# The first column of a scan's input: from VectorE to GpSimd and ScalarE

## The chip, the core and the metric

The kernel runs on one core of a Trainium2 chip. A core has TensorE (PE, matmuls; PEld is its weight load), VectorE (DVE), ScalarE (ACT), GpSimd (POOL) and SyncE (SP), whose queue issues the DMA transfers. Each engine works through its own queue in order. The metric is the time of one execution on the device in microseconds (us).

## The reference

Two layers work on 4 images of 64 x 64 tokens with 256 channels. The first is a Mamba block, the second an SSD block followed by a mixture of 8 experts. What matters here is the recurrence of the first, for 512 channels d and 16 states n:

```python
dt = softplus(dbl[..., :16] @ dt_w.T + dt_b)      # (B, L, 512)
dA = exp(dt[..., None] * A)                       # A = -exp(A_log), (512, 16)
h  = dA * h + (dt * x)[..., None] * B[:, None, :] # over the 4096 tokens of an image
y  = einsum('bdn,bn->bd', h, C)
```

The term that is added in each step is u B with u = dt * x. Where the tokens are cut into chunks, the first step of a chunk also needs dA * h of the last token of the chunk before.

## The kernel before

The program has three stages: *mixers* (both recurrent blocks, 64 chunks of 256 tokens, 16 to an image), *experts* and *turn*. Only the mixers are changed.

**Units.** Channels and states of a chunk are cut into 16 units, unit u = 4 j + f with j over four groups of 128 channels and f over four groups of states. A tile of a unit is 128 partitions (32 channels x 4 states) by four rows of 256 tokens. A unit's steps in `scan` are these:
- `da`, on ACT: four exps of 255 columns each (column 0 of each row stays 0, which starts a row anew), into one of three fixed tiles.
- `ub`, on DVE: the product of `u4` (u, loaded for each j) and row B of `bc4[f]` (B and C, loaded for each f at the chunk's start, five buffers), into a PSUM tile with a single buffer.
- In all chunks but an image's first (60 of 64), a small addition on DVE: `e0[:, :, f]`, what the states bring along, is added to column 0 of the four rows of `ub`. `e0` is made for each j, four units at a time: a product on POOL, exp on ACT, and a product with the last states of the chunk before (`hlast`) on POOL.
- `h`, on DVE: one scan over all 1024 columns.
- `hlast`, on ACT: a copy of the last column of each row of `h`.
- `p`, on POOL: `h` times row C of `bc4[f]`.
- `py`, on PE: the sum over states, added in PSUM to D times the passed-on x, which ACT writes first from `gx`. After two j the result is multiplied on DVE by the other half of `gx`, the gate.

**Order.** Nothing of this is issued as written. `Plan` records each operation with a slot (`k_.at(n)`: n units from the chunk's first) and its dependences, where two uses of parts of a tile that do not meet are independent. `Plan.order` then fills the queues by simulating them with weights written by hand: on each engine, of the operations that are ready and whose buffers have room, the lowest slot goes first. The instructions are issued in that order; the tile framework beneath adds the semaphores. While the scan of chunk i runs, other steps run beside it: `front0` and `mid0` of a later chunk, `tail0`, `front1`, `ssd` and `back1` of earlier ones. `BEHIND` is the planner's delay between an operation and one that depends on it on the same engine.

**Silus.** In the trace an ACT_TABLE_LOAD stands ahead of ACT's Silus and another behind them (x256 in all, mean 1283 ns): `silus` runs the Silus (and a Tanh) of a tile or two and then loads the set with exp and log again. `Plan.acts` records all of these as one operation, which nothing can come between. This happens twice a chunk.

Of the kernel before, what the change touches and what calls it, by code (L numbers as in the profile page):

```python
# [14 lines left out]
AF = mybir.ActivationFunctionType  # L15
ALU = mybir.AluOpType
# [4 lines left out]
P = 128  # L21
T = 256
# [4 lines left out]
KC = C // P  # L27
KD = DI // P
NST = 16
SQ = 4  # L30
# [14 lines left out]
AHEAD = 4  # L45
# [77 lines left out]
class Op:  # L123
    def __init__(self, seq, engine, slot, step):
        self.seq, self.engine, self.slot, self.step = seq, engine, slot, step
        self.calls, self.weight, self.lag = [], 0.0, 0.0
        self.port = self.scan = self.ride = False
        self.behind = self.issued = None
        self.deps, self.users, self.roots = set(), [], []
        self.start = self.end = None  # L130
# [6 lines left out]
class Plan:  # L137
# [4 lines left out]


    SIGNAL = {"DVE": 0.13, "ACT": 0.19, "PE": 0.21, "POOL": 0.12}
    BEHIND = {"DVE": 0.13, "ACT": 0.14, "PE": 0.0, "POOL": 0.13}
    LANES = 8
    SPARE = {}
    PATIENCE = 4.0
# [69 lines left out]
    def act(self, out, src, func, **kw):  # L218
        aps = sum(isinstance(v, Part) or hasattr(v, "ap") for v in kw.values())
        w = 0.06 + self.width(out) / 1130 + 0.09 * aps  # L220
        self.note("ACT", w, self.nc.scalar.activation, (out, src, func), kw, (out,), (src, *kw.values()))

    def copy(self, out, src):
        self.note("ACT", 0.05 + self.width(out) / 1200, self.nc.scalar.copy, (out, src), {}, (out,), (src,))

    def acts(self, weight, calls):

        key = object()
        for f, args, out, src in calls:
            self.note("ACT", weight, f, args, {}, (out,) if out is not None else (), (src,), join=key)  # L230

    def dve(self, name, *args, **kw):
        out, *rest = (*args, *kw.values())
# [41 lines left out]
    def order(self):  # L275
# [19 lines left out]
        lanes, landings = ("SP",), []  # L295
        done = 0
        scan = before = last = shared = None

        def room(op, now):
            for root in op.roots:  # L300
# [9 lines left out]
        while done < len(self.ops):  # L310
            if not events:
                left = [o for o in self.ops if o.start is None and not o.missing][:20]
                raise RuntimeError("no order: " + str([(o.engine, o.slot, [r.ring for r in o.roots]) for o in left]))
            now = heappop(events)
            while events and events[0] <= now:
                heappop(events)
            for e in engines:
                while waiting[e] and waiting[e][0][0] <= now:
                    _, _, op = heappop(waiting[e])
                    insort(could[e], (op.slot, op.seq, op))  # L320
                if free[e] > now or e in lanes and len(landings) >= self.LANES and landings[-self.LANES] > now:
                    continue
                for i, (_, _, op) in enumerate(could[e]):

                    if op.ride and not (scan and now - scan.start < 0.2) and now - op.ready < self.PATIENCE:
                        continue
                    if op.port and port["DVE" if e == "POOL" else "POOL"] > now:
                        continue
                    if room(op, now):
                        break  # L330
                else:
                    continue
                del could[e][i]
                for root in op.roots:
                    if not root.begun:
                        root.begun = True
                        rings[root.ring].append(root)
                op.start, op.end = now, now + op.weight + op.lag
                free[e] = now + op.weight
                heappush(events, free[e])  # L340
                if e in lanes:
                    landings.append(op.end)
                    heappush(events, op.end)
                if op.port:
                    port[e] = free[e]
                if e == "DVE":
                    scan = op if op.scan else None
                    before, last = last, op
                    if op.port:
                        shared = op  # L350
                elif op.ride:
                    op.behind = before if scan and now - scan.start < 0.2 else shared
                for root in op.roots:
                    root.left -= 1
                    root.until = max(root.until, op.end + (0.06 if op.lag else self.SIGNAL[e]))
                    if not root.left:
                        heappush(events, root.until)
                for u in op.users:
                    u.missing -= 1
                    late = op.end + (0.06 if op.lag else (self.BEHIND if u.engine == e else self.SIGNAL)[e])  # L360
                    u.ready = max(u.ready, late)
                    if u.ride and not u.missing:
                        heappush(events, u.ready + self.PATIENCE)
                    if not u.missing:
                        heappush(waiting[u.engine], (u.ready, u.seq, u))
                        heappush(events, u.ready)
                done += 1
# [16 lines left out]
def tile_conv_attn_hybrid(ctx: ExitStack, tc: tile.TileContext, a: dict, out: bass.AP, cap: int, st: int):  # L384
    nc = tc.nc
# [44 lines left out]
    def mixers(es):  # L430
# [29 lines left out]
        m_d = load("m_D")  # L460
# [85 lines left out]
        py = py_p.tile([P, 512], F32, name="py0", tag="py", bufs=1)  # L546
# [16 lines left out]
        SETS = "natural_log_exp_and_others"  # L563
# [3 lines left out]
        r = Plan(tc)  # L567

        def work(shape, tag, bufs=1):
            return r.tile(lambda: wk.tile(shape, F32, name=nm(tag), tag=tag, bufs=bufs), shape, tag, bufs)  # L570
# [86 lines left out]

        def silus(*tiles, gates=0):

            calls = [(nc.scalar.activation, (t, t, AF.Silu), t, t) for t in tiles]  # L660

            calls += [(half_tanh, (t[:, :KC],), t[:, :KC], t[:, :KC]) for t in tiles[:gates]]
            calls.append((nc.scalar.preload_act_table_set, (SETS,), None, None))
            r.acts(sum(0.06 + Plan.width(t) / 1130 for t in tiles) / len(calls) + 2.6 / len(calls), calls)

        def inv_sqrt(dst, src, eps, scale=1.0):

# [164 lines left out]
        for i in range(3):  # L832
            t = wp.tile([P, SQ, T], F32, name=f"da{i}", tag=f"da{i}")
# [7 lines left out]
        def scan(k_):  # L841
            later = k_.c > 0
            k_.hlast = work([P, NG, SQ], "hlast", 2)
            bc4 = []
            for f in range(SQ):

                k_.at(f - AHEAD)
                t = work([P, 2, T], "bc4", SQ + 1)
                for q in range(SQ):
                    r.dma("SP", t[q * R : (q + 1) * R], k_.bc_d[:, f * SQ + q].partition_broadcast(R))  # L850
                bc4.append(t)
            for j in range(KD):

                both = []
                for name, src in (("dt4", k_.dt_d), ("u4", k_.u_d)):
                    k_.at(j * SQ - AHEAD)
                    t = work([P, SQ, T], name, 2)
# [5 lines left out]
                dt4, u4 = both  # L863
                if j % 2 == 0:

                    gx = work([P, 2, 2, T], "gx", 2)
                    for s in range(2):
                        r.dma("SP", gx[:, s], k_.gx_d[s * KD + j : s * KD + j + 2].rearrange("j p l -> p j l"))
                sl = slice(j * SQ, (j + 1) * SQ)
                k_.at(j * SQ - 1)  # L870
                if later:

                    e0 = work([P, SQ, SQ], "e0", 2)
                    r.gps("tensor_tensor", e0, neg_a0[:, sl], dt4[:, :, 0:1].to_broadcast([P, SQ, SQ]), ALU.mult)
                    r.act(e0, e0, AF.Exp)
                    r.gps("tensor_tensor", e0, e0, k_.prev.hlast[:, sl], ALU.mult)
                for f in range(SQ):
                    u = j * SQ + f
                    bc = bc4[f]
# [3 lines left out]
                        r.act(da[:, q, 1:], dt4[:, q, 1:], AF.Exp, scale=neg_a0[:, j * SQ + q, f : f + 1])  # L883
                    k_.at(u)
                    ub = bank_u(SQ, T)
                    r.tt(ub, u4, bc[:, 0, None, :].to_broadcast([P, SQ, T]), ALU.mult)
                    if later:
                        r.tt(ub[:, :, 0], ub[:, :, 0], e0[:, :, f], ALU.add)
                    h = work([P, SQ, T], "h", 3)
                    r.dve("tensor_tensor_scan", h.flat(), da.flat(), ub.flat(), 0.0, ALU.mult, ALU.add)  # L890
                    k_.at(u + 1)
# [5 lines left out]
                    if f == 0:  # L897
                        if j % 2 == 0:
                            py = bank_y(2, T)
                            for i in range(2):  # L900
                                r.act(py[:, i], gx[:, 1, i], AF.Copy, scale=m_d[:, j + i : j + i + 1])
                    for i in range(SQ):
                        r.mm(
                            py[i * R : (i + 1) * R, j % 2],
# [7 lines left out]
                if j == 0:  # L912
                    k_.g = work([P, KD, T], "g0")
                if j % 2 == 1:
                    r.tt(k_.g[:, j - 1 : j + 1], gx[:, 0], py, ALU.mult)

# [22 lines left out]
        def front1(k_):  # L941
# [37 lines left out]
            for k in range(KC):  # L979
                for s in range(NS):  # L980
                    r.transpose(pt[:, k, s * Q : (s + 1) * Q], xn1[:, s, k * P : (k + 1) * P], ident)
            xn = work([P, KC, T], "t")
            r.copy(xn, pt)
            r.tt(ratio, ratio, scale[:, 1], ALU.mult)
            raw = work([P, KD, TAPS - 1 + T], "raw")
# [585 lines left out]
```

## Time and profile before

| What | Value |
|---|---|
| Time, median of 3 runs | 6706.08 us (6697.39 to 6709.94) |
| Profiled execution, its own time | 6706.9 us |
| Its span | 6704.9 us |
| Busy: PE, PEld | 6188.0 us (92%), 4282.6 us (64%) |
| Busy: DVE | 5552.4 us (83%), 7685 instructions |
| Busy: ACT | 4879.5 us (73%), 11999 instructions |
| Busy: POOL | 3295.2 us (49%), 2622 instructions |
| The unit's scan on DVE | x1024, mean 2285 ns |
| The unit's product on DVE | x1024, mean 1250 ns |
| The exps `da` on ACT | x4096, mean 503 ns |
| The copy `hlast` on ACT | x1024, mean 198 ns |
| The product `p` on POOL | x1024, mean 2355 ns |

Busy time is the sum of the durations of an engine's instructions; instructions that follow each other without a wait overlap in the records by a little under 0.1 us on DVE and ACT. A row of a list names the line, the engine, the operation and "written tile <- read tiles". Nearly every row of the mixers has line L373, the line in `Plan.issue` that issues all recorded operations, so rows are told apart by their tiles. "idle before <- releaser" is the time that an engine stood before such an instruction, and what ended it. TensorE's ends are modelled, and a busy PE is not one at its peak.

### The profile page before, as it was taken

What the parts mean: (1) busy time and instruction counts of PE and PEld (TensorE: products, weight loads), DVE (VectorE), ACT (ScalarE), POOL (GpSimd) and SP (SyncE); (2) the same over time, 40 slices, a digit from 0 to 9 for tenths busy, and PEclk for the clock granted to TensorE, in tenths of its full rate; (3) what the DMA queues carried; (4) which work ended last, traced back from release to release, by engine and by line L of the source; (5) the groups of instructions that cost most, each with busy time, mean ns of one, the idle gap of its engine ahead of it and who ended that gap; (6) DMA issues with size and microseconds to landing.
All of it is one profiled execution on the core that took longest, in us unless ns stands there. A gap on an engine that the chain in (4) does not pass through costs nothing. (4 is left out here: it accounts for less than half of the span.)

```text
span 6704.9 us, 111610 instructions
## 1 busy us (share of the span) xinstructions
PE 6188.0 (92%) x37578; PEld 4282.6 (64%) x37578; DVE 5552.4 (83%) x7685; ACT 4879.5 (73%) x11999; POOL 3295.2 (49%) x2622
## 2 busy tenths in 40 slices
PE   7899999999999999999999999999999977999997
PEld 5566666666666666666666666666666646888886
DVE  5999999999999999999999999999999983434443
ACT  5888888888888888888888888888888863333333
POOL 4655555555555555555555555555555552333331
PEclk8999999999999999999999999999999988999998
DMA  6854445455555545455545555555555434555556
GB/s 188 234 149 150 150 147 151 146 151 152 152 153 152 149 145 151 146 150 150 152 148 150 153 153 153 153 153 152 151 153 152 149 102 143 199 199 195 200 197 260
DMA packets 924401, 1078.46 MB, mean 161 GB/s; under 512 B 93537, under 2 KB 895077, under 8 KB 912435
## 3 DMA queue, kind: packets, MB, share of 16 engines
q1 hardware_dynamic: 890002, 842.27, 42.2%
q0 software_dynamic: 29472, 212.28, 8.7%
q10 hardware_dynamic: 4352, 16.78, 0.6%
q8 instruction: 296, 4.85, 0.3%
q14 instruction: 279, 2.28, 0.1%
HBM read 787.00 MB, written 276.76 MB: 159 GB/s over the span
## 5 line engine op out<-in xcount | busy, mean ns | idle before, releaser
L373 POOL TENSOR_TENSOR p<-h,bc 128x1024 f32<-128x1024 f32 x1024 | 2411.3, 2355 | 2008.0 <-DVE ub L373 507.2
L373 DVE TENSOR_TENSOR_SCAN h<-da,ub 128x1024 f32<-128x1024 f32 x1024 | 2339.5, 2285 | 78.1 <-ACT da L373 5.8
L373 ACT ACTIVATE da<-dt,w_m_Alog 128x255 f32<-128x255 f32 x4096 | 1842.6, 503 | 0.0
L373 DVE TENSOR_TENSOR ub<-u,bc 128x1024 f32<-128x1024 f32 x1024 | 1279.7, 1250 | 13.3 <-DMA u<-u_d 5.9
L373 PE MATMUL py<-p,sum 128*32 128x256 f32 x8192 | 662.4, 396 | 183.4 <-POOL p L373 176.8
L373 PE MATMUL b<-t,w_W_in 128*128 128x256 f32 x2304 | 579.6, 392 | 25.6 <-ACT bcs L373 4.9
L373 PEld LDWEIGHTS b<-t,w_W_in 128*128 128x128 f32 x2304 | 418.7, 190 | 189.9 <-ACT raw L373 76.2
L373 PE MATMUL a<-t,w_m_in_w 128*128 128x256 f32 x2048 | 511.3, 393 | 3.1 <-DVE t L373 2.8
L1411 PE MATMUL ph<-xt,w 128*128 128x256 f32 (+1 forms) x2304 | 496.1, 368 | 12.2 <-ACT hid L1413 11.9
L373 PEld LDWEIGHTS py<-p,sum 128*32 128x32 f32 x8192 | 168.9, 108 | 508.0 <-POOL p L373 259.2
L373 PE MATMUL a<-raw,taps_m 128*128 128x256 f32 x2048 | 480.6, 382 | 4.8 <-ACT pre L373 4.8
L1422 PE MATMUL po<-w,hid 128*128 128x256 f32 x2160 | 478.0, 379 | 0.0
L373 PEld LDWEIGHTS a<-t,w_m_in_w 128*128 128x128 f32 x2048 | 371.3, 191 | 145.1 <-issue 73.3
L373 PEld LDWEIGHTS a<-raw,taps_m 128*128 128x128 f32 x2048 | 377.4, 189 | 130.1 <-ACT e L373 39.0
L1411 PEld LDWEIGHTS ph<-xt,w 128*128 128x128 f32 x2304 | 412.3, 190 | 69.5 <-ACT hid L1413 17.9
L1422 PEld LDWEIGHTS po<-w,hid 128*128 128x128 f32 x2160 | 409.7, 190 | 55.3
L373 ACT COPY hlast<-h 128x4 f32<-128x4 f32 x1024 | 202.9, 198 | 278.7 <-DVE h L373 266.1
L1385 DVE CAST number<-rows 128x2 uint32<-128x2 f32 x72 | 12.3, 170 | 450.1 <-DMA tok_d<-fixed,number 437.7
L1383 ACT ACTIVATE tn<-rows 128x256 f32<-128x256 f32 x135 | 77.4, 596 | 401.0 <-DMA rows<-buf_d,row_at 400.3
L1434 POOL DMA_INDIRECT tok_d<-fixed,number x135 | 138.5, 1026 | 402.6 <-DVE fixed L1432 265.0
L373 PE MATMUL c<-cum,after 128*128 128x512 f32 x512 | 321.1, 713 | 14.5 <-ACT dend L373 13.7
L373 ACT ACT_TABLE_LOAD x256 | 328.4, 1283 | 4.7
(237 smaller groups left out, 11312.0 us busy)
## 6 DMA issues: line engine op xcount, KB each, us to landing
dt<-dt_d SPq DMA_DIRECT2D x1024, 128.0 KB, 2.5
u<-u_d SPq DMA_DIRECT2D x1024, 128.0 KB, 2.3
raw<-raw_d SPq DMA_DIRECT2D x1024, 128.0 KB, 3.3
gx_d<-pre SPq DMA_DIRECT2D x64, 1024.0 KB, 4.5
bc<-bc_d SPq DMA_DIRECT2D x1024, 64.0 KB, 2.5
gx<-gx_d SPq DMA_DIRECT2D x256, 256.0 KB, 3.1
raw_d<-raw SPq DMA_DIRECT2D x64, 518.0 KB
dt_d<-mid SPq DMA_DIRECT2D x64, 512.0 KB, 3.2
```

Of the source, the lines that this page charges most:

```text
L373: op.issued = f(*map(placed, args), **{k: placed(v) for k, v in kw.items()})
L1383: act(tn[:, j], rows[:, j, TOK:], AF.Identity, scale=rows[:, j, 1:2], bias=rows[:, j, 2:3])
L1385: nc.vector.tensor_copy(number, rows[:, :, 3])
L1411: mm(ph, w1[:, k, f * P : (f + 1) * P], xt[:, k], start=k == 0, stop=k == KC - 1)
L1422: mm(po[:, j], hid[:, f, j * P : (j + 1) * P], w2[:, f], start=f == 0, stop=f == KF - 1)
L1434: nc.gpsimd.indirect_dma_start(out=tok_d, out_offset=bass.IndirectOffsetOnAxis(ap=number[:, j : j + 1], axis=0), in_=fixed[:, j], in_offse ...
```

## The change

- `e0` is made complete on POOL: for each j, two more operations, the product `u0` of column 0 of B (for all four f) and column 0 of u (for all four rows), and its addition to `e0`. Column 0 of the four B tiles is collected in `b0` by one ACT copy of one column for each f.
- In each unit, ACT copies `e0[:, :, f]` to column 0 of `ub`. DVE's product writes columns 1 to 255 only, and the small addition on DVE is gone.
- `acts` records the Silus, Tanh and the table load as a chain of single operations with their own weights, and `order` lets copies and other operations that need no particular table (`any_set`) come between them.
- `bc4` has six buffers instead of five. `gx` (two buffers of both halves) becomes `pass` and `gate`, one buffer each, of which the gate is loaded at slot 4 j + 3 instead of 4 j - 4. The transposed `xn` of `front1` gets a tile of its own instead of sharing `t`. `BEHIND` of DVE is 0.17 instead of 0.13.

The core of the diff:

```diff
-    BEHIND = {"DVE": 0.13, "ACT": 0.14, "PE": 0.0, "POOL": 0.13}
+    BEHIND = {"DVE": .17, "ACT": 0.14, "PE": 0.0, "POOL": 0.13}
...
-    def acts(self, weight, calls):
-
-        key = object()
-        for f, args, out, src in calls:
-            self.note("ACT", weight, f, args, {}, (out,) if out is not None else (), (src,), join=key)
+    def acts(self, calls):
+
+        ops = []
+        for n, f, args, out, src in calls:
+            op = self.note("ACT", n, f, args, {}, (out,) if out is not None else (), (src,))
+            op.set = ops
+            if ops:
+                ops[0].deps |= op.deps
+                op.deps = {ops[-1]}
+            ops.append(op)
+        ops[0].deps -= set(ops)
...
+                    if e == "ACT" and in_set and not (op.any_set or op.set is in_set):
+                        continue
...
+                if op.set:
+                    in_set = op.set if op is not op.set[-1] else None
...
-                t = work([P, 2, T], "bc4", SQ + 1)
+                t = work([P, 2, T], "bc4", SQ + 2)
...
+                if later:
+                    if f == 0:
+                        b0 = work([P, SQ], "b0", 2)
+                    r.copy(b0[:, f : f + 1], t[:, 0, :1])
...
-                    gx = work([P, 2, 2, T], "gx", 2)
-                    for s in range(2):
-                        r.dma("SP", gx[:, s], k_.gx_d[s * KD + j : s * KD + j + 2].rearrange("j p l -> p j l"))
+                    both = []
+                    for s, name, n in ((1, "pass", -AHEAD), (0, "gate", 3)):
+                        k_.at(j * SQ + n)
+                        t = work([P, 2, T], name)
+                        r.dma("SP", t, k_.gx_d[s * KD + j : s * KD + j + 2].rearrange("j p l -> p j l"))
+                        both.append(t)
+                    passed, gate = both
...
                     r.gps("tensor_tensor", e0, e0, k_.prev.hlast[:, sl], ALU.mult)
+
+                    u0 = work([P, SQ, SQ], "u0", 2)
+                    r.gps(
+                        "tensor_tensor",
+                        u0,
+                        b0[:, None].to_broadcast([P, SQ, SQ]),
+                        u4[:, :, 0:1].to_broadcast([P, SQ, SQ]),
+                        ALU.mult,
+                    )
+                    r.gps("tensor_tensor", e0, e0, u0, ALU.add)
...
                     ub = bank_u(SQ, T)
-                    r.tt(ub, u4, bc[:, 0, None, :].to_broadcast([P, SQ, T]), ALU.mult)
+                    t0 = 0
                     if later:
-                        r.tt(ub[:, :, 0], ub[:, :, 0], e0[:, :, f], ALU.add)
+                        t0 = 1
+                        r.copy(ub[:, :, 0], e0[:, :, f])
+                    r.tt(ub[:, :, t0:], u4[:, :, t0:], bc[:, 0, None, t0:].to_broadcast([P, SQ, T - t0]), ALU.mult)
...
-            xn = work([P, KC, T], "t")
+            xn = work([P, KC, T], "xn")
```

More of the change, by code (lines that the diff above doesn't have):

```diff
@@ L126, in __init__ @@
         self.calls, self.weight, self.lag = [], 0.0, 0.0
-        self.port = self.scan = self.ride = False
+        self.port = self.scan = self.ride = self.any_set = False
+        self.set = None
         self.behind = self.issued = None
@@ L220, in act @@
         w = 0.06 + self.width(out) / 1130 + 0.09 * aps
-        self.note("ACT", w, self.nc.scalar.activation, (out, src, func), kw, (out,), (src, *kw.values()))
+        op = self.note("ACT", w, self.nc.scalar.activation, (out, src, func), kw, (out,), (src, *kw.values()))
+        op.any_set = func in (AF.Identity, AF.Copy)
     def copy(self, out, src):
-        self.note("ACT", 0.05 + self.width(out) / 1200, self.nc.scalar.copy, (out, src), {}, (out,), (src,))
-    def acts(self, weight, calls):
-        key = object()
-        for f, args, out, src in calls:
-            self.note("ACT", weight, f, args, {}, (out,) if out is not None else (), (src,), join=key)
+        op = self.note("ACT", 0.05 + self.width(out) / 1200, self.nc.scalar.copy, (out, src), {}, (out,), (src,))
+        op.any_set = True
+    def acts(self, calls):
[8 more added lines that the diff above has]
+        ops[0].deps -= set(ops)
     def dve(self, name, *args, **kw):
@@ L297, in order @@
         scan = before = last = shared = None
+        in_set = None
         def room(op, now):
@@ L658, in silus, with weight @@
         def silus(*tiles, gates=0):
[L660 to L664, printed above, removed]
+            def weight(t):
+                return 0.06 + Plan.width(t) / 1130
+            load = 1.3
+            calls = [(weight(t), nc.scalar.activation, (t, t, AF.Silu), t, t) for t in tiles]
+            calls += [(weight(t[:, :KC]), half_tanh, (t[:, :KC],), t[:, :KC], t[:, :KC]) for t in tiles[:gates]]
+            calls[0] = (calls[0][0] + load, *calls[0][1:])
+            calls.append((load, nc.scalar.preload_act_table_set, (SETS,), None, None))
+            r.acts(calls)
         def inv_sqrt(dst, src, eps, scale=1.0):
@@ L900, in scan @@
                             for i in range(2):
-                                r.act(py[:, i], gx[:, 1, i], AF.Copy, scale=m_d[:, j + i : j + i + 1])
+                                r.act(py[:, i], passed[:, i], AF.Copy, scale=m_d[:, j + i : j + i + 1])
                     for i in range(SQ):
@@ L914, in scan @@
                 if j % 2 == 1:
-                    r.tt(k_.g[:, j - 1 : j + 1], gx[:, 0], py, ALU.mult)
+                    r.tt(k_.g[:, j - 1 : j + 1], gate, py, ALU.mult)
         def tail0(k_):
```

## The prediction

> **What bounds the kernel now.** I read the busy table in slices first, then the windows of one period, then what DVE waited for, then the timelines of DVE and ACT side by side. The slices show a stage of 5.5 ms (the mixers), in which DVE stands at 9 tenths or more, and a stage of 1.2 ms after it that the change does not touch. One chunk of 256 tokens takes 85.5 us there (64 chunks). Five windows over one such chunk, with the columns window, us, then busy us of PE, PEld, DVE, ACT and POOL, granted clock, DMA share and GB/s:
>
> ```profile
> 3001.50:3015.00 13.50, 13.28 (x84) 10.12 (x84) 13.50 (x21) 9.22 (x27) 5.17 (x3) 1.00 0.45 137
> 3015.00:3027.00 12.00, 9.86 (x57) 6.55 (x56) 11.76 (x27) 8.31 (x27) 10.06 (x10) 1.00 0.88 257
> 3027.00:3056.00 29.00, 27.88 (x191) 17.30 (x193) 27.93 (x32) 28.91 (x77) 18.29 (x14) 1.00 0.50 141
> 3056.00:3072.00 16.00, 13.88 (x85) 7.23 (x81) 13.86 (x16) 13.36 (x25) 7.59 (x6) 0.89 0.54 174
> 3072.00:3087.00 15.00, 15.00 (x114) 11.28 (x114) 14.00 (x20) 12.25 (x29) 5.13 (x4) 1.00 0.25 71
> ```
>
> DVE is full in every window; ACT has a third to spare in the first two and nothing (28.91 of 29.00) in the third. So DVE bounds the stage, and from 3027 to 3056 ACT is as full as DVE. The chain that ended last covers only the final stage and says nothing here. DVE's waits (total us, times, longest) and the group that the change removes (busy us, mean ns, idle before):
>
> ```profile
> DVE cdec L373 <- ACT cdec L373: 79.9, 53, 3.4
> DVE stats L373 <- PE b L373: 74.1, 60, 3.9
> L373 DVE TENSOR_TENSOR ub<-ub,e 128x4 f32<-128x4 f32 x960 | 159.4, 166 | 14.8 <-DVE ub L373 0.5
> ```
>
> The timeline of one unit with the small addition, and of one in the first chunk, which has none (start, us):
>
> ```profile
> 3039.26 1.23 DVE L373 TENSOR_TENSOR ub<-u,bc 128x1024 f32<-128x1024 f32 x1
> 3040.52 0.17 DVE L373 TENSOR_TENSOR ub<-ub,e 128x4 f32<-128x4 f32 x1
> 3040.82 2.29 DVE L373 TENSOR_TENSOR_SCAN h<-da,ub 128x1024 f32<-128x1024 f32 x1
> ...
> 91.36 1.23 DVE L373 TENSOR_TENSOR ub<-u,bc 128x1024 f32<-128x1024 f32 x1
> 92.72 2.29 DVE L373 TENSOR_TENSOR_SCAN h<-da,ub 128x1024 f32<-128x1024 f32 x1
> ```
>
> From the product's end to the scan it is 0.33 us with the addition and 0.13 without. ACT reaches a scan's result like this (scan 3040.82 + 2.29 = 3043.11):
>
> ```profile
> 3041.27 1.91 ACT L373 ACTIVATE pre<-pre 128x2048 f32<-128x2048 f32 x1
> 3043.09 0.40 ACT L373 ACTIVATE bcs<-bcs 128x256 f32<-128x256 f32 x1
> 3043.51 1.28 ACT L373 ACT_TABLE_LOAD   x1
> 3044.80 0.19 ACT L373 ACTIVATE dend<-c 128x24 f32<-128x24 f32 x1
> 3044.89 0.19 ACT L373 COPY hlast<-h 128x4 f32<-128x4 f32 x1
> ```
>
> That hlast copy, which the new ub copy follows in ACT's queue, starts 1.78 us after the scan. Over 936 units, by the two timelines, it starts 0.74 us late on average (median 0.03 for most places in the chunk, 1.4 to 3.2 in four of them); the next scan starts 3.06 us after the last one's end.
>
> **What the skill says.** The Trainium skill, "Perfetto Trace Analysis", Identifying the Most-Contended Engine: occupancy is a fair measure for Vector and Scalar, matmul busy is not for TensorE. It agrees: PE shows 92%, its weight loads 64%, and DVE's waits name DVE as the longer queue. "ScalarE: Activation LUTs", What ACT_TABLE_LOAD costs: a load takes 1283 ns (the trace's mean is 1283), and back-to-back activations overlap by about 93 ns (the trace: 0.08 to 0.10), so I count a 0.198 us copy as 0.10 of ACT's queue and 0.20 to its result. "SBUF — State Buffer", SBUF: two separate sides: a VectorE op with two SBUF inputs and a GpSimd op exclude each other for a whole instruction. It agrees: e on POOL takes 0.22 us and up to 1.29, ub on DVE 1.23 and up to 3.1.
>
> **The change part by part.** Per later chunk (60 of 64):
>
> *Removed from DVE:* 16 additions. Taken start to start they cost 0.20 us where they stood bare (274 of 887), 0.28 with work only ahead of them (168) and 0.12 with work on both sides (444): 155 us per 887, **-2.8 us a chunk**. I take -2.6, since a scan behind its product still needs its 0.13. The product is four columns of 1024 shorter: nothing.
>
> *Added to ACT:* 16 ub copies and 4 b0 copies of about 0.10: +2.0 us of queue. ub has one buffer, so a copy can start only when the scan before is done, and that scan's successor needs it. Before, ACT's work for the scan (da, three buffers) was a unit or two ahead.
>
> *The wait.* The order of the changed program, read with its waits, has what the diff hides. The planner takes column 0 and columns 1 to 255 as disjoint, but the layer beneath takes the two writes to one tile as overlapping: in 581 of 960 units the product waits for the copy (form A), in 370 the copy waits for the product, and the scan for the copy (form B). Nothing runs side by side. By unit of the chunk, B are 0, 1, 11, 12, 14 and 15; the rest are A. A with ACT waiting: hlast 0.03 after the scan, copy 0.10 later, 0.20 long, 0.03 to DVE, so the product starts 0.36 after the scan; other DVE work stands in between in nearly all A units. B: 0.03 + 0.20 + 0.03 = 0.26 in place of 0.33, no loss, but ACT's whole queue stands until the product (1.23) has ended; evictions and da exps are behind it, and PE waits for those.
>
> *Step by step through a chunk,* ACT's queue by the rows da 0.40, eviction of 256 columns 0.36, cum 0.30, decay 0.50, Silu 1.83 and 2.3, load 1.28:
> - Units 11 and 12 (B): 4.7 and 3.0 us of ACT work. ACT stands 0.4 and 0.85 us at the copies; DVE's period stays 3.9 to 4.0.
> - Unit 13 (A): 3.7 us of work (four da, three evictions, three cum, dend) starts only at unit 12's copy; the scan ends 2.4 us after that. The copy is 1.3 us late and the product with it: **+1.4**.
> - 14 and 15 (B, the opened Silu): 4.75 us against 5.3, then 3.7 against 3.6: nothing. Without the opening, the copies would stand 1.8 us behind the second load.
> - Unit 0 (B, after gm, xdt, decay, cdec): about 7.9 us of ACT work against 7 on DVE, part of which waits anyway: +0.5.
> - Unit 1 (B): 5.0 against 5.9, and ACT stands 1.1 until the product ends. Unit 2 (A): py, tanh, py, load, decay, da are 3.7 us against 2.6, the z product covers 0.6: **+1.0**. On the other side cdec moves from where it waited 79.9 us / 60 to behind unit 2's scan: -1.0.
> - Units 3 to 5, 7, 8 (A): 0.4 us and more of DVE work cover the copy.
> - Unit 6 (A): ACT's copy of xn waits for the transposes. Before, that copy (t) started 4.2 us after its input was ready (z 3002.51 + 1.0, t 3007.75). One mid product has left unit 5, so the scan ends earlier and the copy behind xn is 1.4 to 1.7 us late, with row (0.45) to cover: **+1.3**.
> - Units 9 and 10: 0.2 us of cover for 0.36: +0.3.
>
> *POOL:* 480 more operations of 0.22 (u0 and the addition), 107 us on an engine busy half the stage. Each can hold DVE for 0.22 or push p back beside a product: between 0 and 75 us in all; I take 20, +0.3 a chunk. Behind them stand p and the tail copies; u0 of unit 0 needs all four B tiles, which is why bc4 has six buffers: the last can be loaded only after p of unit 13, so 1.8 us of issues and 2.5 us of landing must fit in the two units (8 us) before unit 0. I count nothing; if it fails, ACT stands at b0 with all its queue, up to 2.5 us a chunk (+150).
> *SP:* the same count of transfers. gate is issued seven units later than gx was, three units into its pair and still four ahead of its use (3.1 us to landing): nothing. pass and gate have one buffer each, freed units before: nothing. xn in its own buffer takes away a wait of t behind the other front: 0 to -20 us, nothing taken, as no wait of DVE shows it. The planner's 0.17 for 0.13 is no instruction.
> *Given back:* when DVE is late, PE's results are there earlier. DVE waits for PE 231 us (3.9 a chunk); I take a tenth: -0.4.
>
> Sum: -2.6 - 1.0 + 1.4 + 0.5 + 1.0 + 1.3 + 0.3 + 0.3 - 0.4 = +0.8 us, times 60 = **+48 us** against the profiled execution, 6706.9 (span 6704.9), which is 0.8 above the median of 6706.08: 6755.
>
> **Rivals.** *Faster (0.28):* the copies are covered. If ACT reaches the copy of units 2, 6 and 13 within the DVE work ahead of the product, 3.7 of the waits go and the sum is -2.9 us a chunk: 6532; with half of them, 6644. It decides where ACT's lateness at those three is under 0.6 us. For it: in the old order only 126 of 936 units would have had a copy too late, by 63 us in all, most at the Silus that are now open. Against it: window three, and the 370 waits of ACT that the planner did not count. *ACT becomes the bound (0.12):* each B unit stops ACT for up to 1.2 us; six are 7.4, on 72 busy of 85.5 plus 2, and PE starves behind evictions. If two thirds get through, +5 us a chunk: 7000. Against it: ACT is late at 11, 15 and 0 anyway and stands little there. *No change (0.08).* That the change is not made is excluded: DVE's order has exactly 960 rows fewer.
>
> **How the numbers follow.** The forecast (slower, 0.52): 6755, its own range 6700 to 6870. Half of the faster case and most of the ACT case lie in 6630 to 6890. A difference of 0.2%, 13 us, is about what a measurement of this kernel tells from none: slower 0.52 + 0.12 = 0.64, same 0.08, faster 0.28.
>
> **What would show it.** Right: DVE's product waits for ACT's ub in the list of waits, 150 to 300 us, in units 2, 6 and 13; ACT's ub copies wait for DVE's product in B units, some 200 us; scans without the addition follow 0.26 after the product in B; cdec's wait smaller. Wrong: DVE's waits for ub under 60 us and a period under 84 us (the faster case), or ACT at 9 tenths in all slices and PE's waits for ACT doubled (the ACT case), or ACT's b0 waiting for a transfer.

## The result, and the profile after

The changed kernel takes 6816.16 us (median of 4 runs, 6808.42 to 6821.14) against 6706.42 of the kernel before: a ratio of 1.0165, with a 95% interval of 1.0147 to 1.0182. It is 110 us slower, the way that was forecast and more than twice as much (48). The profiled execution took 6808.42 us (span 6806.7). All of it lies in the mixers: the last scan of a unit started at 5508.6 us before and at 5613.7 now.

The busy line of the page now, and the slices of DVE before, then of DVE and ACT now:

```profile
PE 6239.6 (92%) x37578; PEld 4402.9 (65%) x37578; DVE 5374.0 (79%) x6725; ACT 4998.1 (73%) x13199; POOL 3538.5 (52%) x3102
...
DVE  5999999999999999999999999999999983434443
...
DVE  5889888899988888989888888988888883433443
ACT  5888888888888888888888888888888872333333
```

DVE has lost 178 us of work (5552.4 before) and most of its nines have become eights: the engine that bounded the stage now stands idle more often in it. ACT is busier by 119 us. What DVE waited for (total us, times, longest us; the last row is from before):

```profile
DVE h L387 <- ACT ub L387: 162.3, 301, 2.6
DVE ub L387 <- ACT ub L387: 117.5, 139, 1.8
DVE stats L387 <- PE b L387: 103.9, 53, 3.3
DVE z L387 <- PE b L387: 100.9, 49, 4.5
...
DVE z L373 <- PE b L373: 8.1, 4, 4.5
```

The first two rows are new, 280 us together: scans that wait for ACT's copy (form B) and products that wait for it (form A). In the trace no copy runs beside its unit's product: of the 960, 587 lie ahead of it and 373 behind it. Stats waited 74.1 us before. The groups of the copy on ACT and of cdec on DVE (busy us, mean ns, idle before and releasers):

```profile
L387 ACT COPY ub<-e 128x4 f32<-128x4 f32 x960 | 161.1, 168 | 132.0 <-DVE ub L387 68.1 <-DVE red L387 60.2 <-POOL e L387 3.2
L387 DVE TENSOR_TENSOR cdec<-cdec,cc 128x512 f32<-128x512 f32 x128 | 114.8, 897 | 0.4 <-ACT cdec L387 0.4
```

ACT stands 132 us in front of its copies, nearly all of it until DVE's product has ended (red stands directly behind the product on DVE; the copies that the list puts down to it start 0.04 us after red's end). cdec's 79.9 us of waiting are gone. Units 12 and 13 of one chunk on DVE, then ACT's queue between them (start, us, what, and the idle time ahead of it):

```profile
3062.45 1.23 DVE L387 TENSOR_TENSOR ub<-u,bc 128x1020 f32<-128x1020 f32 x1
3064.06 2.29 DVE L387 TENSOR_TENSOR_SCAN h<-da,ub 128x1024 f32<-128x1024 f32 x1 [0.32 <-ACT ub L387]
3067.81 1.23 DVE L387 TENSOR_TENSOR ub<-u,bc 128x1020 f32<-128x1020 f32 x1 [1.41 <-ACT ub L387]
```

```profile
3062.87 0.19 ACT L387 COPY hlast<-h 128x4 f32<-128x4 f32 x1
3063.79 0.17 ACT L387 COPY ub<-e 128x4 f32<-128x4 f32 x1 [0.74 <-DVE red L387]
3063.89 0.90 ACT L387 ACTIVATE da<-dt,w_m_Alog 128x255 f32<-128x255 f32 x2
...
3066.64 0.98 ACT L387 ACTIVATE cum<-upto,da 128x128 f32<-128x128 f32 x3
3067.52 0.19 ACT L387 COPY hlast<-h 128x4 f32<-128x4 f32 x1
3067.61 0.17 ACT L387 COPY ub<-e 128x4 f32<-128x4 f32 x1
```

In unit 12 ACT is early and stands 0.74 us until the product has ended; DVE then stands 0.32 until the copy is there. What ACT lost there is missing in unit 13: its work of 3.6 us starts only at 3063.89, the scan has long ended (3064.06 + 2.29 = 3066.35), and the product starts 1.41 us late. In these two units each engine waits for the other in turn, and neither gets the time back.

### The profile page after: what moved, and what is told of

It reads as the page before. It is cut to its first block, busy times and chain, and to the rows that moved or that the text cites. A ratio compares the mean times of both kernels' runs of the same rounds, so it can differ in the third digit from the quotient of the medians.

```text
span 6806.7 us, 113175 instructions
## 1 busy us (share of the span) xinstructions
PE 6239.6 (92%) x37578; PEld 4402.9 (65%) x37578; DVE 5374.0 (79%) x6725; ACT 4998.1 (73%) x13199; POOL 3538.5 (52%) x3102
## 5 line engine op out<-in xcount | busy, mean ns | idle before, releaser
L387 DVE TENSOR_TENSOR ub<-u,bc 128x1020 f32<-128x1020 f32 (+1 forms) x1024 | 1268.0, 1238 | 143.2 <-ACT ub L387 117.5
L387 PE MATMUL b<-xn,w_W_in 128*128 128x256 f32 x2304 | 573.6, 390 | 41.4 <-DVE red L387 13.1
L387 PEld LDWEIGHTS b<-xn,w_W_in 128*128 128x128 f32 x2304 | 425.0, 191 | 183.3 <-ACT raw L387 43.9
L387 PE MATMUL a<-t,w_m_in_w 128*128 128x256 f32 x2048 | 494.5, 389 | 5.3 <-ACT raw L387 2.0
L387 ACT ACTIVATE cum<-upto,da 128x128 f32<-128x128 f32 x1024 | 338.0, 397 | 0.7 <-DVE da L387 0.7
```

What stands on the lines that cost most here:

```text
L387: op.issued = f(*map(placed, args), **{k: placed(v) for k, v in kw.items()})
```

## The experiments

The differences below are between medians, the ratios are to the kernel before that ran beside each. The theory on trial, W: the wait between copy and product on one tile is the loss.

**1. No copy, planned anew.** The column is neither copied nor added.

```diff
-                    r.tt(ub[:, :, t0:], u4[:, :, t0:], bc[:, 0, None, t0:]...)    # and the copy before it
+                    r.tt(ub, u4, bc[:, 0, None, :].to_broadcast([P, SQ, T]), ALU.mult)
```

> The changed kernel without the copy into column 0 of ub: the product writes all 256 columns, and what the states bring along is not added (left out of the result); b0, u0 and e0 are still made. Theory W (the wait between copy and product on one tile costs): with the wait goes all of DVE's waiting for ub (280 us in the changed kernel's list of waits), part of which comes back as waits for PE: 6560 to 6640, and DVE's waits for ACT's ub are gone. Rival R (the rest of the change costs: opened Silus, other buffers, POOL's new operations, the planner's 0.17): 6720 to 6800, since without the copy these stay.

Measured: 6506.3 us, ratio 0.9695 (0.9673 to 0.9716). Lower than W's own range: 310 us below the changed kernel. DVE's waits for ub are gone from its list.

**2. The copies aside.** As 1, with ACT's copies into a tile that nobody reads.

```diff
+                        aside = work([P, SQ], "aside", 3)
+                        r.copy(aside, e0[:, :, f])
```

> As the run without the copy, but ACT still makes all 960 copies, into a small tile of their own that nobody reads (what the states bring along is left out of the result). It keeps ACT's work and takes the handover away. Theory W: within 30 us of the run without the copy, 6560 to 6660. Rival A (ACT's added work, some 2 us a chunk, is the cost, as ACT is full in a third of each chunk): at least half of the loss stays, 6700 to 6800.

Measured: 6593.0 us, ratio 0.9832 (0.9816 to 0.9848). It is within W's range but 87 us above run 1, outside the 30. Either ACT's copying costs 87 us or the new plan does; runs 9 and 10 tell which.

**3. DVE places the column.**

```diff
-                        r.copy(ub[:, :, 0], e0[:, :, f])
+                        r.dve("tensor_copy", ub[:, :, 0], e0[:, :, f])
```

> The changed kernel with the column placed by DVE itself (a copy of 4 elements there, in the place of the old addition) and not by ACT. The result is whole. Theory W: no handover between engines, so about the time before, 6680 to 6730. Rival R: the loss stays, 6780 to 6830.

Measured: 6671.6 us, ratio 0.9949 (0.9933 to 0.9966). The same sum made on POOL, with the placing on DVE's own queue, is faster than the kernel before, by a little more than W's range has it.

**4. The old column, the rest of the change.**

```diff
+                    r.tt(ub, u4, bc[:, 0, None, :].to_broadcast([P, SQ, T]), ALU.mult)
+                    if later:
+                        r.tt(ub[:, :, 0], ub[:, :, 0], e0[:, :, f], ALU.add)     # no b0, no u0
```

> The kernel before with the rest of the change: opened Silus, bc4 six deep, pass and gate, xn, 0.17, but the column added on DVE as before, without b0 and u0. Theory W: these are near nothing together, 6680 to 6720. Rival R: 6760 to 6820. A gain below 6680 would say that the opened Silus pay by themselves and that the handover costs even more than the whole difference of 110 us.

Measured: 6664.0 us, ratio 0.9939 (0.9923 to 0.9956). The rest of the change gains 38 us against the kernel before that ran beside it, which is below W's range: the column's new way costs more than the whole difference of 110 us. From here to run 1 it is 158 us, about the price of the old addition on DVE, as far as two plans can be compared. Run 3 is 8 us above run 4: in these two plans POOL's 480 operations and b0 cost next to nothing.

**5 and 6. The planner told of the wait,** copy first in all units, or product first in all units.

```diff
+                        told = r.ops[-1]                 # 5: the copy; 6: the product
...
+                        r.ops[-1].deps.add(told)         # 5: the product; 6: the copy
```

> The changed kernel, with the planner told of the wait: in its record the product of a unit depends on the unit's copy, so all 960 units are of form A and the queues are planned around that. Theory W1 (the loss comes from queues planned as if copy and product ran side by side): a good half of the handover's 223 us (changed kernel less the run with the copies aside) comes back, 6660 to 6740. Theory W2 (the chain scan, copy, product is itself too long with one ub buffer, whoever plans it): 0.33 us more a unit wherever no other DVE work fills it, 6780 to 6880.

> The same told the other way: the copy is recorded behind the product and depends on it, so all 960 units are of form B; ACT need be there only when the product has ended, and the planner knows when. Theory W1: 6640 to 6720, better than A as the product's 1.23 us cover ACT's lateness. Theory W2: ACT stands 0.3 us at each copy and the scan waits 0.26 for it, as much as the old addition cost: 6680 to 6760. Rival (handing over between engines is lost anyway): above 6790.

Measured: 6928.3 us, ratio 1.0329 (1.0309 to 1.0350), and 6753.2, ratio 1.0068 (1.0049 to 1.0088). Copy first in all units is worse than what the planner did unknowing, so W1 falls there. It is worse than W2's range too; W2's chain of scan, copy and product through one buffer is what the list of waits shows, but why it costs even more is not shown. Product first is 63 us better than the changed kernel, in W2's range. The wait does not go away with a plan that knows it; its row is in each list of DVE's waits, of run 5 and of run 6:

```profile
DVE ub L387 <- ACT ub L387: 367.3, 370, 3.6
```

```profile
DVE h L387 <- ACT ub L387: 309.1, 404, 3.7
```

**7 and 8. Opened Silus alone, and the rest without them** (buffers and 0.17; the column as before in both).

> The kernel before with the opened Silus alone. The rest of the change without the column gained 38 us against before. If the opened Silus are what gained (hlast and py no longer stand behind two table loads): 6660 to 6690. If the buffers are: 6695 to 6715.

> The kernel before with the buffers (bc4 six deep, pass and gate, xn) and the planner's 0.17, and the Silus closed as before; the column on DVE as before. The counterpart of the run with the opened Silus alone: 6695 to 6715 if the Silus gained the 38 us, 6660 to 6690 if the buffers and 0.17 did.

Measured: 6654.9 us, ratio 0.9923 (0.9902 to 0.9944), and 6797.9, ratio 1.0137 (1.0117 to 1.0156). The opened Silus gain 53 us by themselves, 5 more than the range for that case. Buffers and delay lose 90, which no theory had.

**9 and 10. The changed kernel's queues kept.** The copy is recorded as in the change, so that the planner makes the same order, and issued into a tile aside (9) or not at all (10); the product writes all of ub.

```diff
-                        r.copy(ub[:, :, 0], e0[:, :, f])
+                        r.note("ACT", 0.05 + SQ / 1200, nc.scalar.copy, (r.placing, e0[:, :, f]), {}, (ub[:, :, 0],), (e0[:, :, f],))
...
+                    r.ops[-1].calls[0] = (nc.vector.tensor_tensor, (ub, u4, bc[:, 0, None, :]..., ALU.mult), {})
```

> The changed kernel's queues, instruction for instruction on all five engines, with the handover alone taken out: ACT's 960 copies go to a small tile of their own, and the product writes all 256 columns of ub (what the states bring along is left out of the result). Until now each run without the handover was also planned anew. Theory W (the wait itself costs): 6560 to 6640, 180 to 250 us below the changed kernel's 6816. Rival P (the changed kernel's plan is what is poor, and the wait only a part): 6680 to 6760, less than half of it.

> The same queues again, with the 960 copies not issued at all. It prices ACT's copying in a fixed order. If ACT's queue is full where the copies stand (the copies aside cost 87 us when planned anew): 40 to 90 us below the run with the same queues. If ACT's slack takes them: within 20 us of it.

Measured: 6551.6 us, ratio 0.9769 (0.9752 to 0.9785), and 6537.8, ratio 0.9752 (0.9735 to 0.9770). By the two traces all engines run the same instructions in the same order, but for where ACT's 960 copies write. So the handover alone costs 6816.2 - 6551.6 = 265 us; run 9 is just below the lower end of W's range, and rival P is out. ACT's copying itself costs about 14 us, so the 87 between runs 1 and 2 were mostly the new plan. The scan's group and four waits of DVE in run 9:

```profile
L387 DVE TENSOR_TENSOR_SCAN h<-da,ub 128x1024 f32<-128x1024 f32 x1024 | 2336.7, 2282 | 54.7 <-ACT da L387 3.9 <-POOL e L387 1.0 <-DVE red L387 0.8
```

```profile
DVE stats L387 <- PE b L387: 107.2, 53, 3.3
DVE row L387 <- issue: 31.5, 31, 2.4
DVE row L387 <- PE c L387: 29.4, 32, 5.9
DVE z L387 <- PE b L387: 12.6, 47, 4.5
```

The scan waits for no ub any more, and of the 100.9 us that z waited for PE only 12.6 are left: that wait came with the handover too. Stats' did not. What made z wait is PE's own work. Here is z with the 16 matmuls ahead of it in two chunks of the changed kernel, and then a window over each group of matmuls (columns as in the prediction, the granted clock third from the end):

```profile
3002.63 4.81 PE L387 MATMUL b<-g,w_m_out_w 128*128 128x256 f32 x16
3007.48 0.69 DVE L387 SCALAR_TENSOR_TENSOR z<-z,b 128x512 f32<-128x512 f32 x1 [1.78 <-PE b L387]
...
3089.54 3.62 PE L387 MATMUL b<-g,w_m_out_w 128*128 128x256 f32 x16
3093.19 0.69 DVE L387 SCALAR_TENSOR_TENSOR z<-z,b 128x512 f32<-128x512 f32 x1
...
3002.60:3007.50 4.90, 4.90 (x18) 4.11 (x17) 3.12 (x4) 4.33 (x11) 2.36 (x1) 0.75 1.00 326
3089.50:3093.20 3.70, 3.70 (x18) 3.23 (x17) 3.61 (x4) 3.02 (x7) 2.22 (x1) 1.00 0.80 267
```

The same matmuls take 4.81 us at a granted clock of 0.75 and 3.62 at the full clock. The trace's record of the clock has stretches at half of it, most of them 3.4 us long. In 48 of the 64 chunks such a stretch touches these matmuls or the 4 us ahead of them, and z waits 96 us there in all; in the other 16 it waits 6. In run 9 a stretch does so in 1 chunk. So part of the 265 us reaches DVE as matmuls that ran at a lower clock. Why the handover puts a stretch there, no run tried.

**11 and 12. Buffers alone, and the delay of 0.17 alone.**

> The kernel before with bc4 six deep, pass and gate, and xn alone (the planner's delay 0.13, Silus closed). With the delay 0.17 these took 6798, 90 us more than before. If the buffers do it (more things are begun early and stand in front): 6760 to 6810. If the delay does it: 6690 to 6730.

> The kernel before with the planner's delay behind a DVE operation 0.17 for 0.13, and nothing else: no instruction changes, only the order. Counterpart of the buffers alone: 6760 to 6810 if the delay does it, 6695 to 6715 if the buffers do.

Measured: 6616.1 us, ratio 0.9868 (0.9852 to 0.9885), and 6724.0, ratio 1.0026 (1.0019 to 1.0034). Both are outside every range that was expected. The buffers alone gain 90 us and are the fastest version here that leaves nothing out; the delay alone loses 18. Both together (run 8) lose 90, so their effects do not add: the delay changes no instruction, and on top of the buffers it costs 182 us.

**13 to 15. The delay back at 0.13:** opened Silus with the buffers; the whole change; the change with the product first and told.

> The old column on DVE with opened Silus and the new buffers, delay 0.13: the rest of the change without its delay of 0.17. The buffers alone took 6616, the Silus alone 6655, both with 0.17 took 6664. If the delay is what spoils the two (it cost 18 us alone and 182 us on top of the buffers): 6560 to 6620, the sum of both gains or better than the buffers. If opened Silus and buffers do not add up: 6620 to 6670.

> The whole change with the delay at 0.13 instead of 0.17. In the changed kernel's own queues the handover costs 265 us. If that holds for another plan too: 6760 to 6860, as slow as the change. If the change is slow by its 0.17, which only reorders: 6640 to 6720.

> The change with the planner told that the copy follows the product, delay 0.13. With 0.17 it took 6753. If the scan's wait for the copy (309 us) stands in any plan: 6720 to 6800, above the buffers alone in any case (6616). If a better plan lets ACT be there in time: 6600 to 6680.

Measured: 6700.2 us, ratio 0.9990 (0.9983 to 0.9996); 6846.8, ratio 1.0205 (1.0188 to 1.0222); 6717.0, ratio 1.0014 (1.0006 to 1.0021). Silus and buffers do not add up either, gaining 53 and 90 alone and 8 together; both expectations of run 13 missed. The change is slow with either delay (6816 and 6847, the latter in the range expected). Against the same kernel with the old column, it loses 6816 - 6664 = 152 us with 0.17 (run 4) and 6847 - 6700 = 147 with 0.13 (run 13), so the loss is no accident of one order. Product first is the better form with either (6753 and 6717, the latter 3 us under its range), and above the buffers alone, as expected.

## Why the prediction was right, and where it failed

The mechanism of the handover was right: waits on both sides of one tile, seen in the order of the changed program. DVE's waits for ub were to be 150 to 300 us and are 280. ACT's waits in front of the copies, some 200, are 128. In the B units 1, 11, 12, 14 and 15 the scan follows its product by 0.30 to 0.46 us (medians), not 0.26. The period was to be above 84 us and is 87.4 (85.5 before). b0 waits 4.8 us for its transfers in all, and POOL's operations cost next to nothing where runs 3 and 4 are compared.

The size was off, +0.8 us a chunk for a measured (6816.2 - 6706.4) / 60 = +1.8. By terms, with the periods of units (from one scan's end to the next) in the changed kernel less those in run 9, as medians over 59 chunks:

| Step of the prediction | Predicted | Measured |
|---|---|---|
| The addition leaves DVE | -2.6 | -2.7 (run 9 against before: 126 us less work and 38 us less in gaps under 0.15 us, over 60) |
| Unit 13 | +1.4 | +1.3 |
| Unit 2 | +1.0 | +1.5 (+0.65 in the 12 chunks at the full clock) |
| Unit 6 | +1.3 | +0.2 |
| Unit 0 | +0.5 | +0.8 |
| Units 9 and 10 | +0.3 | +0.4 |
| Other units, B at 1, 11, 12, 14, 15 | 0 | +0.2 (1, 11, 12 and 15: +0.8; 14: -0.3; 3: -0.2) |
| All waits of the handover | +4.5 | +4.4 (265 us / 60) |
| PE earlier, when DVE is late | -0.4 | no gain: waits for PE are 43 us longer than in run 9, within the +4.4 |
| cdec -1.0, POOL +0.3 | -0.7 | +0.2 (run 9 against before: all of DVE's waits over 0.15 us) |

The sum of the waits held, partly by luck. Unit 6 was put far too high: run 9, without any handover, has nearly the same period there (5.93 against 6.08), as DVE waits 46 us for row in that unit anyway. Against that, the B units were counted at nothing, because 0.26 us took the place of 0.33. That was a slip in the sum: the old 0.33 had already been credited for all 16 units in the -2.6, so the B units owed the difference to 0.13, some 0.8 a chunk for six of them.

The step that failed is the credit of 1.4 us for cdec and for PE's earlier results. Run 9 has the whole change but its handover and stands (6706.4 - 6551.6) / 60 = 2.6 us a chunk below before; the prediction without its waits and without what they give back was -2.6 - 1.0 + 0.3 = -3.3. In the mixers (from the first scan of a unit to the last) DVE's waits over 0.15 us add up to 268 us before and 281 in run 9: those for ACT fell from 85 to 23, cdec's among them, but those for PE rose from 180 to 222, and row now stands 32 us without a releaser that the profile shows. With the handover the waits for PE are 265. So the wait that the new order removed came back at other operations, and lateness shortened none.

What these waits go with can be read from the clock, which the prediction left out although its fourth window had it at 0.89; that window also has DVE at work for 13.86 of 16.00 us, not full. Inside it, before, with one window for the clock:

```profile
3060.33:3063.74 3.41, 3.17 (x7) 0.94 (x8) 3.41 (x7) 2.98 (x7) 0.62 (x1) 0.50 0.46 137
3061.62 2.08 PE L373 MATMUL c<-cum,after 128*128 128x512 f32 x2
3065.54 1.12 PE L373 MATMUL c<-cum,after 128*128 128x512 f32 x2
3068.35 0.69 DVE L373 TENSOR_TENSOR cdec<-cdec,cc 128x512 f32<-128x512 f32 x1 [1.80 <-ACT cdec L373]
```

Here the clock is at half, the first pair of matmuls takes 2.08 us instead of 1.12, ACT's operations on PE's results follow later, and cdec waits for ACT. Of cdec's 80 us, 74 fall in the 36 chunks where the clock was below full in the 6 us ahead, against 6 in the 17 others where it stands in unit 2. The same holds for stats: 68 us in 34 chunks before, 102 in 49 in run 9, and under 5 in the others of either run. The time at half clock in the mixers is 451 us before and 434 in run 9: about the same, but it fell from 162 to 29 us in units 1 and 2 and rose from 84 to 143 in unit 4, where stats waits. With the handover it is 700. No run held the clock fixed, so what it costs alone stays open.

The range held the time. Of the rivals, the faster one (6532 if no copy is late) is near what run 9 shows without the wait, 6552. ACT as the bound is excluded: its own copying costs 14 us (runs 9 and 10), it stands at 8 tenths in the slices of the mixers, and PE's waits for it rose from 115 to 201 us, short of double.

## What to carry to other kernels

Work moved off the bounding engine is not off its path if the result goes back into a single buffer that this engine fills and empties: here some 160 us of additions became 265 us of handover. Read the new program's waits before pricing the new instructions: two engines that write disjoint, interleaved parts of a tile can be put in sequence by the layer that adds semaphores, whatever the planner believes. Price every replaced step once: against the old step or against none, not both. And before crediting a wait that a new order removes, look at what made it: here PE's slower work made DVE wait at the next result instead.

Where a planner orders the queues, an edit's effect includes a new order, which alone moved this kernel by up to 2.7% (runs 8 and 11 differ in one planning constant). To price a mechanism, keep the queues and change only what is issued; the version to keep is found by timing, here the buffers alone, 1.3% faster than before.

## What the runs showed that I had not expected

- TensorE's granted clock differs between orders of the same 37578 matmuls, and not in step with the time: 0.957 before, 0.939 in the changed kernel, 0.935 in run 5, 0.957 in run 9 and 0.972 in run 11, but 0.968 in run 6, which is slower than before. What sets it was not tried.
- Handing over is not one price. In the timeline above DVE's product starts 0.03 us after the copy's end in unit 13, but the scan of unit 12 starts 0.10 after its copy's end. Of the 301 scans that waited for a copy, 243 start 0.10 after it and 56 start 0.03.
- No run gave ub a second buffer, so how much of the 265 us hangs on there being only one is not shown.
- Why 0.17 with the new buffers costs 182 us, and why Silus and buffers do not add, stays open; no run changed the order alone at one place.
